# Attention heads projected out in four groups and context keys computed for both batches at once, in a transformer block on one NeuronCore

## The chip, the core and the metric

The kernel runs on one NeuronCore of a Trainium2 chip. The core has four compute engines with queues of their own: TensorE (matrix products, in the profile PE, and PEld for loading its weights), VectorE (DVE), ScalarE (ACT) and GpSimd (POOL). SyncE (SP) only issues DMA transfers. Work is done from an on-chip memory, and matrix products land in eight PSUM banks, which hold 512 float32 numbers in each of 128 partitions. The metric is device time in microseconds; lower is better.

## The reference

A transformer block in float32: layer norm, self-attention, layer norm, attention to a context, layer norm, a gated feed-forward layer, each with its residual.

```python
h = _layernorm(x, ln1_g, ln1_b)
x = _attention(h, h, sa_wq, sa_wk, sa_wv, sa_wo, sa_bo) + x
h = _layernorm(x, ln2_g, ln2_b)
x = _attention(h, cond_emb, ca_wq, ca_wk, ca_wv, ca_wo, ca_bo) + x
h = _layernorm(x, ln3_g, ln3_b)
p = h @ ff_w1 + ff_b1
a, gate = (p[..., :D_FF], p[..., D_FF:])
h = a * jax.nn.gelu(gate, approximate=False) @ ff_w2 + ff_b2
return h + x
```

`x` is 2 x 1024 x 256 and the context 2 x 154 x 192. There are 16 heads of 64 columns, so attention works on 1024 columns between its input projections and the output projection `wo` (1024 x 256). The feed-forward layer is 1024 wide, with a gate of the same width.

## The kernel before

The work is a fixed order of instructions, written out by hand and not reordered by a scheduler. A **unit** is one pair of heads of one batch. There are 16 units, numbered through batch 0 and then batch 1. Token tiles have 128 rows; a batch has eight.

**Self-attention** takes 8 steps a unit, 128 in all. Step `p` does the scores of 128 queries (`scores`, two tiles `s` of two banks each), their maxima on VectorE, the exponents on ScalarE (`exponents`), an exchange of row statistics by four small DMAs (`exchange`), and for earlier steps the scaling on GpSimd, the transposes on VectorE (`turn_groups`) and the sums with the values (`self_values`, tiles `po`). In steps 0, 1, 4 and 5 of a unit `run_work` puts something from a list `work` on TensorE: the projections of the next unit's queries, keys and values (`pq_sa`, `pk_sa`, `pv_sa`), which need two banks each; what is left of the two banks goes to the list `outs`. A third list, `side`, holds small pieces of the next norm, with the tiles of the residual that each needs (`needs`).

**The output projection** adds up heads in PSUM. `out_piece` (L452) takes one half of a batch's heads, four pairs (`HP = NPAIR // 2`), and one token tile: four products into half a bank, then one VectorE addition of 128 x 256 onto the residual. A half can be projected once its four pairs are done, so `self_beside` (L654) hands out pieces from unit 4 on, two tiles a unit; the last half of batch 1 follows in cross-attention, at its step 5. The head outputs of a half lie in a tile `oT`, of which there are two.

**Cross-attention** has three steps a unit, 48 in all (`cross_first`, tiles `sc`). Beside a unit's steps go the queries of a later unit (`cross_queries`), its keys (`cross_keys`, L700: the product of the context of one batch with one pair's weights, two products of 154 columns, then a copy on ScalarE), for every second unit the context values, two output-projection tiles from unit 6 on (`cross_beside`, L858), and the sums (`cross_values`, tiles `poc`) of two units before. Probabilities go through VectorE transposes and then through eight DMAs that regroup them (`cross_regroup`) before the sums can read them. The output projection's weights `wo` have one buffer; those of cross-attention are loaded when self-attention's last piece is done.

**The feed-forward stage** has 64 slots (`gate_slot`, tiles `pa`; `sum_slot`, tiles `pf`). Beside its first slots run what is left of cross-attention's output projection, half of one half and the whole of the next, and the last norm.

PSUM is given out in three pools of two: `ps_s` for scores, `ps_m` (`mm_tile`) and `ps_o` (`sum_tile`). VectorE's additions wait in a list `adds`, ScalarE's and VectorE's copies out of PSUM in a list `stores`; both are emptied at fixed places in each step.

Of the kernel before, what the change touches and what calls it, by code (L numbers as in the profile page):

```python
# [13 lines left out]
P = 128  # L14
# [4 lines left out]
def tile_transformer_block(ctx: ExitStack, tc: tile.TileContext, a: dict, out: bass.AP):  # L19
# [10 lines left out]
    HP = NPAIR // 2  # L30
# [105 lines left out]
    def load_weights(kind, pr, what):  # L136
        if kind == "sa" or what == "q" or what == "k":
            wsl[kind, pr, what] = load_slice(
                f"{kind}_w{what}", pr * P, P, HR if kind == "sa" or what == "q" else CC)
        elif pr % 2 == 0:  # L140
            wsl[kind, pr, what] = load_slice(f"{kind}_w{what}", pr * P, VC, CC)
# [4 lines left out]
    def load_ahead_parts():  # L146
# [10 lines left out]
        def chunk(i):  # L157
            nc.sync.dma_start(out=wo["sa"][:, i, :], in_=w["sa_wo"][i * P:(i + 1) * P, :])

        pieces = ([lambda t=t: tile_of_x(t) for t in tile_order("sa")]  # L160
                  + [lambda i=i: chunk(i) for i in range(NPAIR)])
        slots = [u * 2 * SH + n for u in range(1, HP + 1) for n in (0, 1, 4, 5)]
# [21 lines left out]
    nc.gpsimd.memset(ctxT, 0.0)  # L184

# [131 lines left out]
    def norm_beside(kind, b):  # L317
# [12 lines left out]
        for k in range(NT // n + 3):  # L330
            tiles = tile_order(kind)[k * n:(k + 1) * n]
            needs = [(after, b, half, t) for half in range(2) for t in tiles if after]
# [119 lines left out]
    def out_piece(kind, b, half, t):  # L452

        o = oT[kind, b, half]
        py = spare["out"](f"py_{kind}{b}_{half}_{t}")
        for i in range(HP):
            nc.tensor.matmul(  # L457
                py[:, :D], lhsT=o[:, i, t * P:(t + 1) * P], rhs=wo[kind][:, half * HP + i, :],
                start=(i == 0), stop=(i == HP - 1),
            )  # L460
        xs = xt[b, t // GT][:, t % GT, :]

        def add():
            nc.vector.tensor_tensor(xs, py[:, :D], xs, ALU.add)  # L464
            added.add((kind, b, half, t))

        add.adds = True
        return add

# [184 lines left out]
    def self_beside(ui):  # L654
# [9 lines left out]
        if ui >= HP:  # L664
            ob, oh = divmod((ui - HP) // HP, 2)
            t0 = (ui % HP) * 2
            out_pieces("sa", ob, oh, tile_order("ca")[t0:t0 + 2])
        if ui == 1:
            norm_beside("sa", 1)
        if ui in (HP, HP + 2):  # L670
            add_biases("sa", (ui - HP) // 2)
# [3 lines left out]
    def load_ahead(p):  # L675

        ui, n = divmod(p, 2 * SH)
        for what in "qkv":
            at = {"q": 2, "k": 3, "v": 2 * SH - 1}[what] + 3 * (ui == 0 and what != "v")
            if n != at:  # L680
                continue
# [4 lines left out]
        if p in (SA - 3, SA - 2):  # L686
            load_weights("ca", units[p - SA + 4][1], "kq"[p - SA + 3])
# [6 lines left out]
    def cross_queries(b, pr, m=P, bank=mm_tile):  # L694
        q = qk["ca", b, pr, "q"] = p2.tile([P, S], F32, tag="QT", name=f"q_ca{b}_{pr}")
# [4 lines left out]
    def cross_keys(b, pr, bank=mm_tile):  # L700
        k = qk["ca", b, pr, "k"] = p2.tile([P, S], F32, tag="KT", name=f"k_ca{b}_{pr}")
        pk = bank(f"pk_ca{b}_{pr}")
        for c in range(2):
            nc.tensor.matmul(
                pk[:, :T], lhsT=wsl["ca", pr, "k"][:, c, :],
                rhs=ctxT[:, c, b * TP:b * TP + T], start=(c == 0), stop=(c == 1),
            )
        return lambda: nc.scalar.copy(k[:, :T], pk[:, :T])
# [36 lines left out]
    def cross_pieces(b, pr):  # L745

        return [costing(2, lambda: cross_queries(b, pr, KB)), costing(1, lambda: cross_keys(b, pr)),
                costing(1, lambda: context_values(b, pr))]

    def cross_first(c):  # L750
# [4 lines left out]
        q, k = qk["ca", b, pr, "q"], qk["ca", b, pr, "k"][:, :T]  # L755
# [102 lines left out]
    def cross_beside(ui):  # L858
# [3 lines left out]
        if ui > HP + 1:  # L862
            ob, oh = divmod((ui - HP - 2) // HP, 2)
            t0 = ((ui - HP - 2) % HP) * 2
            out_pieces("ca", ob, oh, (t0, t0 + 1))
        if ui == NU - 4:
# [99 lines left out]
    with tc.manual_schedule():  # L966
# [57 lines left out]
        for p in range(SA):  # L1024
# [10 lines left out]
            flush(adds)  # L1035
            if late:
                late()
            if later and (p < 2 * SH * HP or p % (2 * SH) in (2, 4, 6)):
# [5 lines left out]
            if h == 0 or hg < LAG:  # L1044

                run_work(2 if p < SA - SH else 1, h % 2 or h == 0, sum_tile)
                if p == LAG:
                    load_weights("sa", units[1][1], "v")
            else:
                run(lambda: self_values(h - 1, hg - LAG))  # L1050

        for c in range(CA):
# [5 lines left out]
            if c == SH + 1:  # L1058
                out_pieces("sa", B - 1, 1, tile_order("ca"))
                outs.append(lambda: load_out("ca"))  # L1060
# [12 lines left out]
            elif n == 2:  # L1073
# [116 lines left out]
```

## Time and profile before

| | |
|---|---|
| median of 3 runs | 1136.88 us (1136.82 to 1140.38) |
| profiled execution | 1138.26 us, its span 1136.5 us |
| TensorE busy | 1109.5 us (98%) |
| VectorE busy | 841.2 us (74%) |
| ScalarE busy | 632.0 us (56%) |
| GpSimd busy | 681.2 us (60%) |
| self-attention | 0 to about 717 us |
| cross-attention | about 717 to 936 us |
| feed-forward | about 936 us to the end |

The profile is of one execution. Its span runs from the first to the last instruction; the time of a run has a little more around it. "L457" is line 457 of the kernel. A float32 product is two TensorE instructions, so the four products of an output-projection tile are eight in the profile. A tile is named by its program name without its number (`py_sa` is an output-projection tile of self-attention). [...]

### The profile page before, as it was taken

Reading aid. Unit: us, or ns where it says so; the run is one execution under the profiler, and the core shown is the slowest. Engines: PE = TensorE matmul, PEld = TensorE weight load, DVE = VectorE, ACT = ScalarE, POOL = GpSimd, SP = SyncE. Lnnn points to the kernel's source line nnn. Section 1 sums busy time; section 2 is a strip of 40 time slices with the busy share of each in tenths; the row PEclk is TensorE's granted clock in tenths of the full one; section 3 lists DMA queues with packets and bytes.
Section 4 is the critical chain, followed back from the end, with each engine's and each line's share of the span. In section 5 each row is a group of like instructions: output and inputs, shape, how many; then the busy total and the mean of one; then the engine's idle time right before and its main releaser. Section 6 shows DMA issues by size and latency. Waiting matters only on the chain.

```text
span 1136.5 us, 36749 instructions
## 1 busy us (share of the span) xinstructions
PE 1109.5 (98%) x14372; PEld 689.9 (61%) x14372; DVE 841.2 (74%) x1203; ACT 632.0 (56%) x2046; POOL 681.2 (60%) x1584
## 2 busy tenths in 40 slices
PE   8999999999999999999999999999999999999998
PEld 6444444545545545445455454675777767888887
DVE  4889999898898999899998889767666773222222
ACT  4666666666765666666677666646555552021111
POOL 2777777878777777777777767757554553040000
PEclk9999999999999999999999999999999999999999
DMA  2222122201111111111111010166755542000000
GB/s 83 62 53 49 40 49 50 54 18 40 37 25 41 31 31 45 31 32 40 26 37 40 22 32 12 39 160 167 173 123 123 123 88 57 10 10 10 19 10 19
DMA packets 104911, 59.94 MB, mean 53 GB/s; under 512 B 32090, under 2 KB 95522, under 8 KB 104738
## 3 DMA queue, kind: packets, MB, share of 16 engines
q1 hardware_dynamic: 103506, 56.93, 21.0%
q8 instruction: 114, 1.87, 0.7%
q10 hardware_dynamic: 1232, 0.66, 0.2%
q14 instruction: 59, 0.48, 0.1%
HBM read 27.91 MB, written 2.10 MB: 26 GB/s over the span
## 4 chain that ended last, share of the span: by engine, by line
PE 79%; ACT 6%; DVE 4%; DMA 4%; POOL 3%; SPq 2%; issue 2%; DVEq 0%; POOLq 0%; ACTq 0%
PE po L526 16%; PE s L479 16%; PE pa L921 9%; PE py_sa L457 5%; PE pf L944 5%; PE py_ca L457 5%; ACT p L490 4%; PE pk_sa L353 4%; PE pq_ca L353 4%; PE pv_sa L384 4%; PE poc L839 4%; PE pq_sa L353 3%; PE sc L760 2%; SPq L500 2%; DVE st L641 2%; DMA st<-st 2%
## 5 line engine op out<-in xcount | busy, mean ns | idle before, releaser
L490 ACT ACTIVATE p<-s,st 128x512 f32<-128x512 f32 x512 | 344.8, 686 | 203.2 <-DVE st L641 197.3
L591 POOL TENSOR_SCALAR p<-p,rd,ee 128x512 f32<-128x512 f32 x512 | 385.6, 767 | 45.2 <-DVE rd L587 44.2
L641 DVE TENSOR_REDUCE st<-s 128x2 f32<-128x1024 f32 x256 | 301.2, 1218 | 32.6 <-PE s L479 20.9
L605 DVE STREAM_TRANSPOSE pT<-p 128x1024 f32<-128x1024 f32 x256 | 302.2, 1218 | 0.3 <-POOL p L591 0.3
L479 PE MATMUL s<-k_sa,q_sa 64*32 64x512 f32 x4096 | 252.6, 594 | 13.1 <-ACT p L490 12.5
L526 PE MATMUL po<-pT,v_sa 64*64 64x256 f32 x4096 | 235.8, 379 | 0.4 <-DVE pT L605 0.4
L526 PEld LDWEIGHTS po<-pT,v_sa 64*64 64x64 f32 x4096 | 150.4, 133 | 109.0 <-issue 32.0
L787 POOL TENSOR_SCALAR p<-p,rden 128x154 f32<-128x154 f32 x256 | 96.8, 398 | 89.4 <-DVE rden L784 89.0
L479 PEld LDWEIGHTS s<-k_sa,q_sa 64*32 64x32 f32 x4096 | 66.1, 106 | 135.9 <-issue 62.4
L776 ACT ACTIVATE p<-sc,neg 128x154 f32<-128x154 f32 x256 | 95.9, 401 | 87.3 <-DVE rden L784 82.0
L930 DVE SCALAR_TENSOR_TENSOR u<-pa,cols,gate 128x256 f32<-128x256 f32 x64 | 30.9, 483 | 121.8 <-ACT gate L927 121.8
L921 PE MATMUL pa<-hT_ln,wf 128*128 128x256 f32 x512 | 120.7, 379 | 0.0
L927 ACT ACTIVATE gate<-pa,cols 128x256 f32<-128x256 f32 x64 | 30.3, 474 | 155.3 <-PE pa L921 153.6
L921 PEld LDWEIGHTS pa<-hT_ln,wf 128*128 128x128 f32 x512 | 96.8, 190 | 13.5 <-DVE o_ca L852 0.4
L490 ACT ACTIVATION_READ_ACCUMULATOR p<-s,st 128x1 f32 x512 | 103.9, 203 | 0.0
L384 PEld LDWEIGHTS pv_sa<-sa_wv,hT_ln 64*128 64x128 f32 x1024 | 59.0, 188 | 17.4 <-DMA st<-st 7.5
L514 POOL TENSOR_TENSOR zz<-ee,st 128x8 f32<-128x8 f32 x128 | 25.9, 202 | 66.0 <-ACT ee L512 66.0
L944 PE MATMUL pf<-wf,u 128*128 128x256 f32 x256 | 64.7, 379 | 0.0
L384 PE MATMUL pv_sa<-sa_wv,hT_ln 64*128 64x128 f32 x1024 | 62.8, 276 | 0.6 <-ACT v_sa L393 0.6
L457 PE MATMUL py_ca<-ca_wo,o_ca 128*128 128x256 f32 x256 | 60.9, 387 | 0.9 <-DVE x L464 0.8
L457 PE MATMUL py_sa<-sa_wo,o_sa 128*128 128x256 f32 x256 | 59.5, 385 | 0.0
L765 DVE TENSOR_REDUCE neg<-sc 128x6 f32<-128x924 f32 (+1 forms) x48 | 47.9, 999 | 14.4 <-PE sc L760 14.4
(87 smaller groups left out, 1245.1 us busy)
## 6 DMA issues: line engine op xcount, KB each, us to landing
wf<-pT_ca SPq DMA_DIRECT2D x128, 128.0 KB, 2.4
st<-st SPq DMA_DIRECT2D x512, 1.0 KB, 1.8
v_sa<-v_sa SPq DMA_DIRECT2D x32, 256.0 KB, 3.5
sa_wq<-in_L_xattn_sa_wq_dram SPq DMA_DIRECT2D x32, 128.0 KB, 3.0
sa_wk<-in_L_xattn_sa_wk_dram SPq DMA_DIRECT2D x32, 128.0 KB, 3.0
sa_wv<-in_L_xattn_sa_wv_dram SPq DMA_DIRECT2D x32, 128.0 KB, 3.0
ca_wq<-in_L_xattn_ca_wq_dram SPq DMA_DIRECT2D x32, 128.0 KB, 3.0
wf<-in_L_xattn_ff_w_dram SPq DMA_DIRECT2D x12, 256.0 KB, 3.9
```

Of the source, the lines that this page charges most:

```text
L353: nc.tensor.matmul(pq[r][f:f + m, at:at + n], lhsT=wt[own, c, f:f + m], rhs=h[own, c, t0:t0 + n], start=(c == 0), stop=(c == NH - 1), tile ...
L384: nc.tensor.matmul(pv[r][:, i * P:(i + 1) * P], lhsT=h[own, c, i * P:(i + 1) * P], rhs=wt[own, c, :], start=(c == 0), stop=(c == NH - 1), ...
L457: nc.tensor.matmul(py[:, :D], lhsT=o[:, i, t * P:(t + 1) * P], rhs=wo[kind][:, half * HP + i, :], start=(i == 0), stop=(i == HP - 1),)
L479: nc.tensor.matmul(sc[a4 * KB:(a4 + 1) * KB, j, :], lhsT=q[r, c:c + KB], rhs=k[r, h * HB:(h + 1) * HB], start=True, stop=True, tile_positi ...
L490: nc.scalar.activation(pr[:, j, :], sc[:, j, :], AF.Exp, bias=st[:, 0, 0, i, j:j + 1], accum_out=st[:, 0, 1, i, j:j + 1],)
L526: nc.tensor.matmul(po[a2][j * DH:(j + 1) * DH, :QH // 2], lhsT=v[r, t, e, j * DH:(j + 1) * DH], rhs=pT[r, j * NK + n, :], start=(t == 0 an ...
L591: nc.gpsimd.tensor_scalar(pr[:, j, :], pr[:, j, :], rd[:, c:c + 1], ee[:, 0, c:c + 1], op0=ALU.mult, op1=ALU.mult,)
L605: nc.vector.transpose(halves[h][:, :, c:c + KB], groups.pop(0).rearrange("p j (n k) -> p (j n) k", k=KB))
L641: nc.vector.tensor_reduce(st[:, 0, 0, i, :], sc[i], AX.X, ALU.max, negate=True)
L787: nc.gpsimd.tensor_scalar(pr_[:, j, i, :T], pr_[:, j, i, :T], rden[:, j, i:i + 1], 1.0, op0=ALU.mult, op1=ALU.mult,)
L921: nc.tensor.matmul(pa[:, half, :TF * P], lhsT=w1[:, c, half * DF + f * P:half * DF + (f + 1) * P], rhs=h[:, c, t0 * P:(t0 + TF) * P], star ...
L944: nc.tensor.matmul(sums[blk][i][:, :D], lhsT=sums[blk, "u"][:, f, i * P:(i + 1) * P], rhs=w2[:, f, :], start=(f == 0), stop=(f == NF - 1),)
```

## The change

The heads of a batch are projected out in four groups of two pairs in place of two halves of four. A piece covers two token tiles, each with two products, side by side in one bank, and one VectorE addition of 128 x 512. Pieces begin at unit 2 of self-attention and at unit 4 of cross-attention; of batch 1 one group is left for cross-attention's step 5, and two for the feed-forward slots 0 and 5. In self-attention VectorE does at most one waiting addition a step. The first two weight rows of `wo` are loaded ahead of half of batch 1's token tiles.

The context's keys are computed once a pair for both batches (two products of 320 columns, one ScalarE copy into a tile that stays), in step 5 of self-attention's units 1 to 8; cross-attention no longer computes keys. Their weights are loaded once a pair, in step 6 of a unit (step 4 of unit 0), into a single buffer.

At the end of cross-attention the pieces of its last unit run in the first of its steps. The load of cross-attention's `wo` stands in the last step of unit 2, ahead of that step's regrouping.

```diff
-    HP = NPAIR // 2
+    NQ = 4
+    HP = NPAIR // NQ
...
-        if kind == "sa" or what == "q" or what == "k":
...
+        if (kind, what) == ("ca", "k"):
+            wsl[kind, pr, what] = load_rows(
+                wpool, "ck", f"ca_wk_{pr}", w["ca_wk"][:, pr * P:(pr + 1) * P], CC)
...
-        pieces = ([lambda t=t: tile_of_x(t) for t in tile_order("sa")]
-                  + [lambda i=i: chunk(i) for i in range(NPAIR)])
-        slots = [u * 2 * SH + n for u in range(1, HP + 1) for n in (0, 1, 4, 5)]
+        tiles = [lambda t=t: tile_of_x(t) for t in tile_order("sa")]
+        chunks = [lambda i=i: chunk(i) for i in range(NPAIR)]
+        pieces = tiles[:4] + chunks[:HP] + tiles[4:] + chunks[HP:]
+        slots = [u * 2 * SH + n for u in range(1, 5) for n in (0, 1, 4, 5)]
...
+    kT = const.tile([P, NPAIR, B * TP], F32, tag="kT", name="kT")
...
-    def out_piece(kind, b, half, t):
+    def out_piece(kind, b, g, t):
 
-        o = oT[kind, b, half]
-        py = spare["out"](f"py_{kind}{b}_{half}_{t}")
-        for i in range(HP):
-            nc.tensor.matmul(
-                py[:, :D], lhsT=o[:, i, t * P:(t + 1) * P], rhs=wo[kind][:, half * HP + i, :],
-                start=(i == 0), stop=(i == HP - 1),
-            )
-        xs = xt[b, t // GT][:, t % GT, :]
+        o = oT[kind, b, g]
+        py = spare["out"](f"py_{kind}{b}_{g}_{t}")
+        for e in range(2):
+            for i in range(HP):
+                nc.tensor.matmul(
+                    py[:, e * D:(e + 1) * D], lhsT=o[:, i, (t + e) * P:(t + e + 1) * P],
+                    rhs=wo[kind][:, g * HP + i, :], start=(i == 0), stop=(i == HP - 1),
+                )
+        xs = xt[b, t // GT][:, t % GT:t % GT + 2, :].rearrange("p t d -> p (t d)")
 
         def add():
-            nc.vector.tensor_tensor(xs, py[:, :D], xs, ALU.add)
+            nc.vector.tensor_tensor(xs, py, xs, ALU.add)
...
+    def out_order(kind):
+
+        return [t for t in tile_order("ff" if kind == "ca" else "ca") if t % 2 == 0]
...
         if ui >= HP:
-            ob, oh = divmod((ui - HP) // HP, 2)
+            ob, og = divmod((ui - HP) // HP, NQ)
             t0 = (ui % HP) * 2
-            out_pieces("sa", ob, oh, tile_order("ca")[t0:t0 + 2])
+            out_pieces("sa", ob, og, out_order("sa")[t0:t0 + 2])
...
+        if n == (4 if ui == 0 else 6) and ui < NPAIR:
+            load_weights("ca", ui, "k")
...
-    def cross_keys(b, pr, bank=mm_tile):
-        k = qk["ca", b, pr, "k"] = p2.tile([P, S], F32, tag="KT", name=f"k_ca{b}_{pr}")
-        pk = bank(f"pk_ca{b}_{pr}")
+    def context_keys(pr):
+
+        pk = sum_tile(f"pk_{pr}")
         for c in range(2):
             nc.tensor.matmul(
-                pk[:, :T], lhsT=wsl["ca", pr, "k"][:, c, :],
-                rhs=ctxT[:, c, b * TP:b * TP + T], start=(c == 0), stop=(c == 1),
+                pk[:, :B * TP], lhsT=wsl["ca", pr, "k"][:, c, :], rhs=ctxT[:, c, :],
+                start=(c == 0), stop=(c == 1),
             )
-        return lambda: nc.scalar.copy(k[:, :T], pk[:, :T])
+        return lambda: nc.scalar.copy(kT[:, pr, :], pk[:, :B * TP])
...
         if ui > HP + 1:
-            ob, oh = divmod((ui - HP - 2) // HP, 2)
+            ob, og = divmod((ui - HP - 2) // HP, NQ)
             t0 = ((ui - HP - 2) % HP) * 2
-            out_pieces("ca", ob, oh, (t0, t0 + 1))
-        if ui == NU - 4:
+            out_pieces("ca", ob, og, out_order("ca")[t0:t0 + 2])
+        if ui == NU - 5:
             norm_beside("ff", 0)
...
-            flush(adds)
+            if adds:
+                adds.pop(0)()
...
+                ui, n = divmod(p, 2 * SH)
+                if n == SH + 1 and 0 < ui <= NPAIR:
+                    run(lambda: context_keys(ui - 1))
...
             if c == SH + 1:
-                out_pieces("sa", B - 1, 1, tile_order("ca"))
-                outs.append(lambda: load_out("ca"))
+                out_pieces("sa", B - 1, NQ - 1, out_order("sa"))
...
-            elif n == 2:
-                for i, what in ((2, "k"), (1, "v")):
-                    if 1 < ui + i < NU:
-                        load_weights("ca", units[ui + i][1], what)
-            if c == 0:
-                run(lambda: cross_keys(*nxt))
+            elif n == 2 and nxt and ui:
+                load_weights("ca", nxt[1], "v")
             flush(adds)
             then = cross_first(c)
-            if n == 1 and ui > 1 and nxt:
-                run(lambda: cross_keys(*nxt, sum_tile))
-                stores.insert(0, stores.pop())
...
                 run(lambda: self_values(2 * NU - 1, 1))
-                run(lambda: cross_keys(*nxt, sum_tile))
             elif n == 0 and ui:
                 if nxt:
                     run(lambda: cross_queries(*nxt))
+                else:
+                    run_work(2, 0)
                 run_work(0, 1)
...
-                run_work(0, 1, sum_tile if ui == HP - 1 else None)
-                if len(outs) > 2:
+                run_work(0, 1, sum_tile if ui == HP + 1 else None)
+                if c == SH + 1:
                     run_work(2, 0)
+                elif ui == HP:
+                    load_out("ca")
...
             if k == 0:
-                out_pieces("ca", B - 1, 0, range(NT - 2 * TF, NT))
-            if k == 1:
-                run_work(2, 0)
-                flush(adds)
+                out_pieces("ca", B - 1, NQ - 2, out_order("ca"))
...
             if k == len(CG) + 2:
-                out_pieces("ca", B - 1, 1, range(NT))
+                out_pieces("ca", B - 1, NQ - 1, out_order("ca"))
...
-            run_work(2, 1)
+
+            run_work(0 if k == 1 else 2, 1)
```

## The prediction

> **What bounds the kernel now.** I read the page first, then TensorE per unit, then its matmuls in order of time. The page (busy time; then tenths in 40 slices):
>
> ```profile
> PE 1109.5 (98%) x14372; PEld 689.9 (61%) x14372; DVE 841.2 (74%) x1203; ACT 632.0 (56%) x2046; POOL 681.2 (60%) x1584
> ...
> PE   8999999999999999999999999999999999999998
> ...
> DVE  4889999898898999899998889767666773222222
> ```
>
> TensorE (PE) is busy everywhere and VectorE (DVE) nearly so for the first 60%; averages don't say which one sets the pace. So the windows of single self-attention units, cut at their first score matmul: units 1, 2, 3, then 10 and 13 (window, PE, PEld, DVE, ACT, POOL busy, clock, DMA):
>
> ```profile
> 60.87:103.91 43.04, 40.92 (x708) 20.19 (x704) 38.96 (x45) 27.24 (x83) 32.01 (x72) 1.00 0.21 52
> 103.91:148.57 44.66, 41.37 (x709) 20.17 (x705) 39.75 (x46) 28.56 (x87) 33.42 (x77) 1.00 0.19 44
> 148.57:192.19 43.62, 41.27 (x713) 19.84 (x709) 39.75 (x46) 29.96 (x91) 32.31 (x71) 1.00 0.19 46
> ...
> 455.07:498.51 43.44, 43.44 (x724) 22.69 (x720) 39.67 (x48) 28.29 (x82) 32.68 (x73) 1.00 0.15 34
> 586.58:630.61 44.03, 44.03 (x729) 23.14 (x725) 39.07 (x44) 30.20 (x88) 32.85 (x75) 1.00 0.15 33
> ```
>
> Units 1 to 3 leave PE idle; from unit 4 on it never stops. The chain of waits through unit 10 (start, us, what):
>
> ```profile
> 455.14 1.88 PE s L479 x32
> 457.02 3.43 PE pq_sa L353 x64
> ...
> 467.32 3.61 PE po L526 x64
> ...
> 478.30 3.77 PE pv_sa L384 x64
> ...
> 483.95 3.65 PE py_sa L457 x16
> ```
>
> A unit is eight score sets (8 x 1.88), four po pieces (4 x 3.61), pq and pk (3.43 each), pv (3.77) and two out-projection tiles (3.65): 43.8, against 43.44 measured. So here every microsecond of matmul counts. Units with a norm's transposes take 0.58 more (44.03).
>
> [...] The row that decides is the sum of pieces that equals the period, with no gap: in this order of work PE is full. [...]
>
> Cross-attention and the start of the feed-forward stage, PE in order of time (start, us, matmul, idle before it and who ended it):
>
> ```profile
> 794.93 0.86 PE L839 MATMUL poc<-wf,v_ca 64*64 64x256 f32 x10 [1.73 <-DVE hT_ln L282]
> ...
> 846.17 0.79 PE L704 MATMUL pk_ca<-ctxT,ca_wk 96*128 96x154 f32 x4
> 846.80 3.62 PE L457 MATMUL py_ca<-ca_wo,o_ca 128*128 128x256 f32 x16
> ...
> 925.92 1.06 PE L760 MATMUL sc<-k_ca,q_ca 64*128 64x154 f32 x12 [1.80 <-ACT p L776]
> ...
> 927.67 5.02 PE L457 MATMUL py_ca<-ca_wo,o_ca 128*128 128x256 f32 x16
> ...
> 942.80 3.72 PE L457 MATMUL py_ca<-ca_wo,o_ca 128*128 128x256 f32 x16 [0.81 <-DVE x L464]
> ```
>
> PE runs without gaps from unit 6 to unit 14 (27.0 us for two units), has gaps around units 4 and 5 and between 924 and 950, and is full again (170.00 of 170.00 us) from 963 to 1133.
>
> **The change, part by part.** A py matmul costs 0.216 (3.45 for x16), a pk_ca set of four 0.63 (846.17 to 846.80).
>
> *Self-attention, out-projection from unit 2.* Units 2 and 3 now get two pieces of two tiles, 16 instructions, 3.65 us each, and one value projection in place of two halves. They then hold what unit 13 holds. With the keys (below) each is 44.03 + 1.08 = 45.1, against 44.66 and 43.62: **+1.9**. Their weight rows are brought forward in SP's queue by half a unit and batch 1's later tiles back by as much; each is still at least half a unit ahead of its reader.
>
> *Context keys.* Four instructions with N=320 in place of 154. At 256 columns one takes 0.216, so 0.27 here: 1.08 a unit, in units 1 to 8 at step 5. Unit 1 has idle PE (2.1 us, at just these steps): 0. Units 4 to 8: **+5.4**. ScalarE's copy (294 ns at 154, 372 at 256, so some 430) goes ahead of the next step's exponents; po, queued behind it for the bank, starts only after 1.9 us of scores. One 96 KB load of SP a unit, at a step that had none, falls between two exchanges; the wait on its single buffer ends a step earlier.
>
> *Adds twice as wide.* 64 as before. DVE issues two of 256 in 0.72 and a 1024-wide reduce in 1.18, so 512 takes about 0.63: two take 1.26, not 0.72, one in each of steps 6 and 7 rather than both in 6. DVE waits 0.38 and 0.54 for the denominators in those steps, which covers them; the next q projection, queued behind the bank of the second add, starts 0.3 after its end. I take **+0.2**, ends 0 and 7 (0.5 in each of 14 units if that cover is missing).
>
> *Cross-attention, units 0 and 1.* Of the two key sets, the one at 717 lies ahead of a po at 728.16 that waits 0.41 for DVE's transposes: 0. The one at 736: **-0.7**.
>
> *Units 2 to 5.* Out go four key sets (-2.5) and four single sa tiles of the old last half (-7.2: x16 in unit 2's third step, x16 in unit 3). In come two ca groups' tiles in units 4 and 5 (+6.9), which fill the waits there (783 and 795: split poc runs of 3.6 and 5.1 us instead of 2.75: -3.75). New in unit 3: the 1 MB ca_wo load now stands just ahead of the eight regrouping DMAs that poc waits for. SP needs 5.3 to 6.3 us to issue those eight; the packets show ca_wo filling the DMA engines for 4.5 us. Unit 3 has only 5.9 us of PE work between two poc runs (sc 0.7, sc 0.9, pq 3.4, sc 0.9), so poc waits: between 0 and 4.5, I take +2.3. Sum **-4.3**.
>
> *Units 6 to 14.* Nine key sets: **-5.7**. SP loses 0.5 a unit of issue. Two odd units with a transpose find the first, wider add late for poc's bank: **+0.8** (0 to 2).
>
> *Unit 15 and the start of the feed-forward.* Unit 15's two pieces now run in its first step, into the 1.80 gap. Gone too should be the 0.81 and 0.61 (949.88) behind the crowd of single tiles at its second slot. And the clock: the 16 py instructions at 927.67 took 5.02 instead of 3.45. The granted clock in stretches of 3.4 us:
>
> ```profile
> 923.20:926.60 3.40, 1.60 (x25) 1.37 (x24) 3.40 (x8) 1.70 (x9) 2.22 (x7) 1.00 0.94 200
> 926.60:930.00 3.40, 3.40 (x16) 2.79 (x15) 3.15 (x8) 3.40 (x19) 2.53 (x10) 0.57 0.49 104
> ```
>
> A stretch with PE at 1.60 of 3.40 and then half a clock. [...] The row shows the fall right after a half-idle stretch, so I count the 1.57 too. Together 4.8, less 0.6 for new waits (the exponents of the last steps, the regrouping, 7.6 us from release to landing, now with 6.4 us of work ahead of unit 14's poc): **-4.2**.
>
> *Feed-forward.* Out-projection instructions fall from 96 to 64; PE is full: 32 x 0.216 = **-6.9**. These 32 are the ones that units 2 and 3 took in, passed on by way of cross-attention.
>
> Sum: 1.9 + 5.4 + 0.2 - 0.7 - 4.3 - 5.7 + 0.8 - 4.2 - 6.9 = **-13.5**. Made the other way: matmul work on the path is nearly unchanged (14 key sets out, 9.0; eight in, 8.6; out-projection equal), so almost all is idle PE filled: 9 in units 1 to 3, the rest around cross-attention's ends. The profiled execution took 1138.26 with a span of 1136.5; the median of the runs is 1136.88, and I take the difference from that: **1123.4 us**.
>
> **Rivals.**
> - *Cross-attention has a floor below PE*: without the keys, the exponent chain, the regrouping or SP sets the pace. For it: SP is issuing nearly all the time from 783 to 800. Against: DVE is at 17.6 of 27.1 and ACT at 15.9 in the steady pairs. Two thirds of nine key sets lost, and a fall of the clock in unit 3's new wait: +7, 1130.5.
> - *The additions to self-attention hide*[...]: 7.5 less, 1116. Against: the sum of pieces.
> - *Work is only moved, no idle time is filled*: the new places wait as the old did, and 9.0 - 8.6 remain: 1136.5.
> - *Slower: VectorE becomes the pace of self-attention.* Units 1 to 3 took 43.0 to 44.7 with PE idle, bound by the loop score, maximum, exponent. If the wider add, in front of the next maximum, stretches that loop, PE waits in all 14 units with out-projection. At 0.96 us a unit the gain is gone; at 1.26, 1141. Against: in unit 12 (with a norm) the exponents end 0.8 to 2.4 us before the scores that need their bank; only at step 0 of unit 8 have I seen 0.24.
>
> **How the numbers follow.** Likeliest 0.58 (own range 1119 to 1128, from the ends of the waits above); floor 0.16; hidden 0.10; only moved 0.08; slower 0.08. A change under 0.3% (3.4 us) can't be told from none. Faster 0.84, same 0.08, slower 0.08. The range, 1115 to 1131, holds the first three but for their edges and leaves out the last two.
>
> **What would show it.** Units 2 and 3 at 45.1, 4 to 8 at 44.5 to 45.3, 9 to 15 unchanged; cross-attention pairs at 25.8, not 27.0; a gap on poc near 760 with ca_wo ahead of it; no half clock near 927; py out of the feed-forward after two slots instead of four. Wrong if units 9 to 15 grow (the adds), if pairs stay at 27, or if the end of cross-attention keeps its gaps.

## The result, and the profile after

| | before | after |
|---|---|---|
| median, us | 1137.90 (1136.82 to 1140.38) | 1130.72 (1130.03 to 1131.45) |
| ratio, with 95% interval | 1 | 0.9934 (0.9914 to 0.9954) |
| profiled execution: time, span | 1138.26, 1136.5 | 1130.48, 1128.7 |

The changed kernel is 7.2 us faster (0.66%, 0.5 to 0.9% by the interval). When it was run again on another chip, beside the kernel before, it took 1130.86 us and the ratio was 0.9923 (0.9907 to 0.9940). The kernel before took 1136.88 us in the runs that the prediction started from, and its median was 1137.9 to 1139.9 in the later comparisons; so ratios are compared below where kernels were run on different chips. The predicted 1123.4 us was too low. The measured 1130.7 lies inside the range of 1115 to 1131, by 0.3 us, and outside the 1119 to 1128 that the likeliest reading allowed itself.

The page of the changed kernel: busy times, then TensorE's and VectorE's tenths of 40 slices.

```profile
PE 1110.2 (98%) x14340; PEld 690.0 (61%) x14340; DVE 856.5 (76%) x1205; ACT 631.2 (56%) x2032; POOL 681.0 (60%) x1584
...
PE   8999999999999999999999999899999999999998
...
DVE  4889889898888988999989989977767875312222
```

TensorE is as busy as before (1110.2 us, it was 1109.5) in a span 7.8 us shorter: the gain is idle time, as the prediction said. One slice in the middle, the 26th (705 to 734 us), now shows 8. That is where something went wrong.

The windows of self-attention units 1, 2, 3, 6, 7, 10 and 13 (window, its length, busy time of PE, PEld, DVE, ACT, POOL, the granted clock, DMA share and rate):

```profile
62.39:105.16 42.77, 41.92 (x712) 20.16 (x708) 38.96 (x45) 27.59 (x84) 31.66 (x70) 1.00 0.20 50
105.16:151.20 46.04, 45.60 (x728) 24.45 (x724) 40.74 (x47) 29.22 (x88) 33.42 (x78) 1.00 0.20 48
151.20:196.36 45.16, 45.16 (x732) 24.63 (x728) 40.80 (x48) 30.42 (x89) 32.87 (x75) 1.00 0.19 46
...
287.59:332.70 45.11, 45.11 (x732) 23.90 (x729) 39.45 (x43) 29.26 (x87) 33.94 (x75) 1.00 0.15 35
332.70:377.22 44.52, 44.52 (x728) 23.48 (x724) 39.44 (x43) 28.25 (x83) 33.92 (x76) 1.00 0.15 35
466.07:509.64 43.57, 43.57 (x724) 23.62 (x721) 40.46 (x48) 28.38 (x83) 33.35 (x77) 1.00 0.14 33
597.91:641.94 44.03, 44.03 (x729) 23.15 (x725) 39.44 (x44) 30.33 (x89) 32.87 (x74) 1.00 0.15 33
```

Units 2 and 3 had TensorE idle for 3.3 and 2.4 us and are full now but for 0.44 us in unit 2, yet they are longer (44.66 and 43.62 before). Units 6 and 7 carry one key set each (two products, four instructions) and are 1.08 and 1.0 us longer (44.03 and 43.51 before). Unit 13 is what it was.

TensorE in order of time through cross-attention and the first feed-forward slots (start, us, line, matmul, shapes, count; in brackets the idle time before it and who ended it):

```profile
773.10 0.65 PE L851 MATMUL poc<-wf,v_ca 64*64 64x256 f32 x4 [1.56 <-DMA wf<-pT_ca]
774.22 0.86 PE L851 MATMUL poc<-wf,v_ca 64*64 64x256 f32 x10 [0.47 <-DMA wf<-pT_ca]
...
776.63 0.87 PE L851 MATMUL poc<-wf,v_ca 64*64 64x256 f32 x10 [0.65 <-ACT p L788]
...
927.43 3.72 PE L463 MATMUL py_ca<-ca_wo,o_ca 128*128 128x256 f32 x16
...
935.81 1.99 PE L933 MATMUL pa<-hT_ln,wf 128*128 128x256 f32 x8 [0.20 <-ACT p L788]
...
961.54 3.62 PE L463 MATMUL py_ca<-ca_wo,o_ca 128*128 128x256 f32 x16
...
968.45 3.62 PE L463 MATMUL py_ca<-ca_wo,o_ca 128*128 128x256 f32 x16
```

The first three lines are unit 3's wait for the regrouped probabilities. The other lines are the end of cross-attention: the out-projection at 927 takes 3.72 us where it took 5.02, the gap of 1.80 us ahead of it is gone, and the last four pieces, two to a run of 16 instructions, stand in feed-forward slots 5 and 6. The granted clock over that end, and over 3.4 us near 717:

```profile
924.00:927.40 3.40, 3.40 (x60) 2.44 (x52) 2.13 (x5) 0.00 (x0) 0.00 (x0) 1.00 0.42 92
927.40:930.80 3.40, 3.40 (x18) 2.96 (x16) 3.40 (x8) 2.52 (x13) 3.04 (x9) 1.00 0.80 174
717.00:720.40 3.40, 3.40 (x36) 0.58 (x40) 3.15 (x5) 1.35 (x5) 2.17 (x7) 0.60 0.01 1
```

The clock stays at 1.00 at the end of cross-attention. It falls near 717 instead, in the last unit of self-attention, which nothing in the prediction touched: 0.60 is the mean of this window, and the trace has the clock at 0.50 from 717.68 to 721.09. Below, such a stretch is called a half clock.

The whole difference of the two profiled spans, cut at the same instructions:

| stage | before, us | after, us | difference | predicted |
|---|---|---|---|---|
| start, to the first scores | 17.67 | 17.96 | +0.29 | 0 |
| self-attention, units 0, 1 | 86.24 | 87.20 | +0.96 | 0 |
| units 2, 3 | 88.27 | 91.20 | +2.93 | +1.9 |
| units 4 to 8 | 219.44 | 225.37 | +5.93 | +5.4 |
| units 9 to 14 | 263.20 | 264.22 | +1.02 | +0.2 |
| unit 15 | 42.90 | 43.74 | +0.84 | 0 |
| cross-attention, units 0, 1 | 23.73 | 22.63 | -1.10 | -0.7 |
| units 2 to 5 | 56.83 | 54.00 | -2.83 | -4.3 |
| units 6 to 14 | 124.87 | 120.21 | -4.66 | -4.9 |
| unit 15, and slots 0 to 4 | 36.93 | 31.44 | -5.49 | -4.2 |
| slots 5 to 62 | 168.63 | 161.72 | -6.91 | -6.9 |
| slot 63 to the end | 7.75 | 8.99 | +1.24 | 0 |
| sum | 1136.5 | 1128.7 | -7.8 | -13.5 |

Not every row here is the change, and rows move between executions. When the changed kernel was profiled again, the last stretch took 7.76 us, unit 0 took 43.54 (in the profile above it has a half clock near 35 us) and unit 9 took 43.48. But units 10 and 11 were longer there, units 2 to 8 took 1.5 us more, and the span was 1128.9 us all the same. So a row of less than about 1 us can't be booked to a cause from one profile, while some 5.7 us are missing in both. The experiments went after the parts that have places and names.

### The profile page after: what moved, and what is told of

Its sections match the earlier page's. It is cut to its first block, busy times and chain, and to the rows that moved or that the text cites. A ratio compares the mean times of both kernels' runs of the same rounds, so it can differ in the third digit from the quotient of the medians.

```text
span 1128.7 us, 36667 instructions
## 1 busy us (share of the span) xinstructions
PE 1110.2 (98%) x14340; PEld 690.0 (61%) x14340; DVE 856.5 (76%) x1205; ACT 631.2 (56%) x2032; POOL 681.0 (60%) x1584
## 4 chain that ended last, share of the span: by engine, by line
PE 86%; ACT 4%; DVE 3%; DMA 3%; POOL 2%; SPq 1%; issue 1%; DVEq 0%; POOLq 0%; ACTq 0%
PE po L536 18%; PE s L489 18%; PE pa L933 10%; PE py_ca L463 5%; PE pf L956 5%; PE py_sa L463 5%; PE pk_sa L358 4%; PE pq_ca L358 4%; PE pq_sa L358 4%; PE pv_sa L389 4%; PE poc L851 4%; PE sc L772 3%; ACT p L500 3%; DMA st<-st 2%; DVE st L651 1%; SPq L510 1%
## 5 line engine op out<-in xcount | busy, mean ns | idle before, releaser
L463 PEld LDWEIGHTS py_sa<-sa_wo,o_sa 128*128 128x128 f32 x256 | 47.3, 190 | 17.8 <-issue 7.0
```

The source lines that it names most:

```text
L463: nc.tensor.matmul(py[:, e * D:(e + 1) * D], lhsT=o[:, i, (t + e) * P:(t + e + 1) * P], rhs=wo[kind][:, g * HP + i, :], start=(i == 0), st ...
```

## Experiments

My theory after reading the two traces: the groups do what they should, and the keys don't pay. In self-attention they cost their full matmul time and a wait on top, and by leaving the last unit they opened a gap there that halves the clock. Rivals: the groups themselves fell short; the loss is the load of cross-attention's output weights in unit 3; the keys hide and the loss is elsewhere.

### The groups alone

The context keys go back to where they were, one batch at a time: two sets in self-attention's last unit, fourteen beside cross-attention.

```diff
...
-                ui, n = divmod(p, 2 * SH)
-                if n == SH + 1 and 0 < ui <= NPAIR:
-                    run(lambda: context_keys(ui - 1))
...
+            if n == 1 and ui > 1 and nxt:
+                run(lambda: cross_keys(*nxt, sum_tile))
+                stores.insert(0, stores.pop())
...
+                run(lambda: cross_keys(*nxt, sum_tile))
```

> Output projection in four groups, keys computed in cross-attention as before. If the gain is idle TensorE time filled by out-projection (units 2 and 3, the ends of cross-attention) and the keys are a trade of 9 us against 9 us, this kernel is as fast as the changed one or faster: units 4 to 8 back at 43.5 to 44.0 us, a pair of cross-attention units back at 27.0, the key matmuls at the end of self-attention back; sum about 1128 to 1132. If the keys are what brings the gain, it loses most of it: 1135 or more.

Measured: 1131.24 us (1127.35 to 1132.52), ratio 0.9922 (0.9895 to 0.9948): what the whole change gives, within intervals of half a per cent. The profiled execution, at 1127.35 us, was the fastest of its four. The windows of self-attention units 2, 3, 6 and 7 of this kernel:

```profile
103.58:147.54 43.96, 43.96 (x724) 23.40 (x720) 39.85 (x46) 28.26 (x85) 33.18 (x76) 1.00 0.19 45
147.54:192.09 44.55, 44.55 (x728) 24.27 (x724) 41.51 (x49) 30.79 (x92) 33.18 (x77) 1.00 0.18 45
...
280.34:324.37 44.03, 44.03 (x728) 23.14 (x724) 39.45 (x43) 29.15 (x86) 33.95 (x76) 1.00 0.14 33
324.37:367.82 43.45, 43.45 (x725) 22.73 (x721) 39.45 (x43) 27.58 (x82) 33.99 (x76) 1.00 0.15 34
```

Out-projection in units 2 and 3, two pieces each, costs -0.7 and +0.9 us: it lies in what was idle. Units 6 and 7 are back at the length before. Against this kernel the keys of both batches cost 11.9 us in self-attention (711.75 from the first scores to cross-attention's first, 699.84 here) and save 10.2 in cross-attention (22.63 + 54.00 + 120.21, against 23.78 + 57.21 + 126.04). Of the 11.9 us, 1.6 are in unit 0, which holds no keys and had the half clock near 35 us (the mean clock from 34 to 40 us was 0.72, and 1.00 with the groups alone); without it the cost is 10.3. So the keys bring nothing that can be seen, and the gain is that of the rest: the groups, with the changes at the end of cross-attention and in the loads, which no run takes apart.

### The keys twice

Each set of key products is done twice. The second pass starts the sum anew, since its first product has `start` set, so the keys are the same and only work is added.

```diff
-        for c in range(2):
+        for c in (0, 1, 0, 1):
```

> The changed kernel with every key product of self-attention issued twice (8 instructions in place of 4; the result is the same). If TensorE is full in these units, units 2 to 8 grow by 1.08 us each and unit 1 by less: 7 to 8.6 us more in all. If the additions hide[...], the time doesn't change.

Measured: 1135.46 us, ratio 0.9969 (0.9959 to 0.9979), 4 to 5 us above the changed kernel and less than the 7 to 8.6 expected. Its units 6 and 7:

```profile
288.64:335.24 46.60, 46.60 (x736) 24.61 (x732) 39.45 (x43) 29.40 (x87) 34.09 (x76) 1.00 0.15 33
335.24:380.84 45.60, 45.60 (x732) 24.24 (x728) 39.45 (x43) 28.07 (x83) 34.16 (x76) 1.00 0.15 34
```

Four more instructions lengthen unit 7 by 1.08 us (44.52 to 45.60) and unit 8 by the same; unit 6 by 1.5. PEld is at 24.24 of 45.60 us in unit 7, just over half: weight loading was idle for the other half, and the added products cost their full length all the same. This refutes the prediction's rival that the additions hide. Over units 1 to 8 the doubling costs 6.5 us (359.4 to 365.9) and not 8.6: in units 2 to 5 it covers a wait, the next point, and unit 1 had idle time.

### The keys one step earlier

With the groups alone, steps 5 and 6 of units 2 to 8 take 5.53 and 5.49 us. In the changed kernel step 5 takes 6.61, the 1.08 of the four instructions more. But in units 2, 4 and 5 step 6 grew too, to 6.53, 6.25 and 5.75. TensorE at these steps of unit 2, and ScalarE in unit 4:

```profile
138.01 1.24 PE L717 MATMUL pk<-ctxT,ca_wk 96*128 96x320 f32 x4
139.18 1.95 PE L489 MATMUL s<-k_sa,q_sa 64*32 64x512 f32 x32
141.06 0.65 PE L536 MATMUL po<-pT,v_sa 64*64 64x256 f32 x4
142.11 3.67 PE L536 MATMUL po<-pT,v_sa 64*64 64x256 f32 x60 [0.40 <-ACT kT L721]
```

```profile
231.68 1.09 ACT L266 ACTIVATE xn_ln<-x,off_ln,rstd_ln 128x256 f32<-128x256 f32 x2 [1.69 <-DVE off_ln L252]
232.68 0.40 ACT L721 COPY kT<-pk 128x320 f32<-128x320 f32 x1
```

po needs the bank that pk holds, and the copy that frees it is done late: in ScalarE's queue it stands behind the norm's scaled rows, which wait 1.69 us for VectorE's offsets. The units bear this out. From the start of the key products to that of the copy it takes 3.64, 2.65, 3.36 and 2.86 us in units 2 to 5, and step 6 is longer by 1.04, 0.05, 0.76 and 0.26: each time by what goes beyond 2.6 us. In units 6 and 7, with no such rows ahead of the copy, it takes 1.3 us and step 6 stays at 5.49. The experiment puts the keys at step 4, where no rows of a norm follow.

```diff
-                if n == SH + 1 and 0 < ui <= NPAIR:
+                if n == SH and 0 < ui <= NPAIR:
```

> The changed kernel with the context keys one step earlier, in step 4 of units 1 to 8, so that their copy on ScalarE is not queued behind the norm's scaled rows. If that queue makes po wait in step 6 (0.40, 0.76 and 0.26 us in units 2, 4 and 5), those waits vanish and 1.5 us are gained in units 2 to 5. If the bank is late for another reason, they stay or move to step 5.

Measured: 1128.29 us, ratio 0.9903 (0.9883 to 0.9923). The same po in this kernel:

```profile
138.31 1.95 PE L489 MATMUL s<-k_sa,q_sa 64*32 64x512 f32 x32
140.19 3.68 PE L536 MATMUL po<-pT,v_sa 64*64 64x256 f32 x64
```

It runs as one piece, and step 6 is 5.49 us in units 2 to 8. Units 2 to 5 fall from 182.4 to 180.7 us in all; in units 7 and 8, where no wait was, nothing is gained (44.72 us each, 44.52 before). The time fell by some 2.5 us, with intervals that overlap; the steps carry the verdict.

### The output weights after the regrouping

In unit 3 of cross-attention the 1 MB load of `ca_wo` stands in SP's queue ahead of the eight transfers that regroup the probabilities (start, us, line, transfer; of the changed kernel):

```profile
764.95 0.54 SPq L121 DMA_DIRECT2D ca_wo<-in_L_xattn_ca_wo_dram  x1
765.58 6.94 SPq L832 DMA_DIRECT2D wf<-pT_ca  x8
```

Here it is issued behind them:

```diff
-                elif ui == HP:
-                    load_out("ca")
             cross_regroup(c)
+            if c == len(CG) * HP + 2:
+                load_out("ca")
```

> The changed kernel with the 1 MB load of cross-attention's output weights issued just behind the regrouping transfers of that step, not ahead of them. If that load holds up the regrouping, the wait of poc in unit 3 (about 3.8 us in all near 771 to 778) falls to under 1 and the kernel gains 2.5 to 3.5 us. If the wait is a floor of SP's issue or of the chain of exponents, unit 3 stays at 13.0 us and the time doesn't change.

Measured: 1130.53 us, ratio 0.9923 (0.9904 to 0.9943): no gain. Unit 3 falls from 13.01 to 10.74 us, and unit 4 grows from 14.36 to 16.48, for what now stands behind the load is late:

```profile
780.33 3.91 PE L358 MATMUL pq_ca<-hT_ln,ca_wq 64*128 64x512 f32 x15 [1.22 <-DMA ca_wq<-in_L_xattn_ca_wq_dram]
```

The load costs some 2 us whichever transfer stands behind it. It has to be cut up or be early.

### The output weights in eight rows

Both stages' weights use one tile. A row of 128 KB is loaded as soon as self-attention has read its row for the last time: six beside its last units, two behind the regrouping in cross-attention.

```diff
-        wo["sa"] = const.tile([P, NPAIR, D], F32, tag="wo", name="sa_wo")
+        wo["sa"] = wo["ca"] = const.tile([P, NPAIR, D], F32, tag="wo", name="sa_wo")
...
+        rows_at = [12 * 2 * SH, 12 * 2 * SH + 1, 14 * 2 * SH, 14 * 2 * SH + 1, SA - 4, SA - 3]
...
-                elif ui == HP:
-                    load_out("ca")
             cross_regroup(c)
+            if c in (len(CG) * HP + 2, len(CG) * HP + 4):
+                load_row(NPAIR - 2 + (c - len(CG) * HP) // 4)
```

> The changed kernel with cross-attention's output weights loaded in eight rows of 128 KB as self-attention's last groups free them, six of them before cross-attention, into the same tile. If the 1 MB of data is what holds up the regrouping and then the query weights, poc no longer waits near 771 and no later wait takes its place: units 3 and 4 take 24.5 to 25.5 us together in place of 27.4, 2 to 3 us gained. If the issuing queue or the exponents set that stretch, it stays at 27.

Measured: 1129.15 us, ratio 0.9905 (0.9890 to 0.9920). SP issues the same eight transfers in 5.28 us, not 6.94, and what is left of the wait in unit 3 is another's:

```profile
765.89 5.28 SPq L832 DMA_DIRECT2D wf<-pT_ca  x8
```

```profile
774.83 1.35 PE L851 MATMUL poc<-wf,v_ca 64*64 64x256 f32 x14 [0.88 <-ACT q_ca L373]
```

Units 3 and 4 together take 25.40 us, against 27.37 in the changed kernel's first profile and 26.99 when it was run again: the load's price in the changed kernel is 1.6 to 2.0 us. Behind it a wait of 0.88 us on ScalarE's copy of the queries comes to light, where 0.65 on ScalarE's exponents stood before; the expectation had no later wait.

### The changed kernel again, and the context values one step later

The last unit of self-attention, in the changed kernel, against the kernel before (one fence each):

```profile
709.51 1.99 PE L733 MATMUL pv_ca<-ca_wv,ctxT 96*128 96x256 f32 x8
...
716.96 3.30 PE L489 MATMUL s<-k_sa,q_sa 64*32 64x512 f32 x32 [2.88 <-ACT p L500]
720.19 4.10 PE L536 MATMUL po<-pT,v_sa 64*64 64x256 f32 x64
```

```profile
700.51 1.09 PE L479 MATMUL s<-k_sa,q_sa 64*32 64x512 f32 x16 [1.34 <-ACT p L490]
...
705.54 1.09 PE L479 MATMUL s<-k_sa,q_sa 64*32 64x512 f32 x16 [0.68 <-ACT p L490]
```

The list of pieces that beside this unit's steps go to TensorE had a key set in it before (at 698). Without it the context values come up one step earlier, and step 5 has nothing between two sets of scores: one gap of 2.88 us in place of 1.34 and 0.68. After it 32 score instructions take 3.30 us and not 1.95: that is the half clock at 717. This experiment puts a piece that does nothing where the keys were, so that the values return to step 5; beside it the changed kernel ran once more.

```diff
-        return [costing(2, lambda: cross_queries(b, pr, KB)), costing(1, lambda: context_values(b, pr))]
+        return [costing(2, lambda: cross_queries(b, pr, KB)), costing(1, lambda: None),
+                costing(1, lambda: context_values(b, pr))]
```

> The changed kernel with the context values put back to step 5 of unit 15, where they stood before the keys that were ahead of them were taken away (an empty piece takes their place). If the single TensorE gap of 2.88 us in that unit, which the advance of the values made out of smaller gaps, is what halves the clock near 717, then the gap splits into pieces of about 2 us and less, the half clock there is gone, unit 15 takes 42.9 us or less in place of 43.7 and the time falls by 0.8 to 1.8. If the half clock has another cause it stays.

> The changed kernel itself, beside the next three on one chip, as their base: 1130 to 1131 us.

Measured: 1130.72 us, ratio 0.9917 (0.9902 to 0.9932), against 1130.86 and 0.9923 (0.9907 to 0.9940) of the changed kernel again: the same. The edit missed what it was for. The gap is shorter, but not split as it was before, and the half clock is still there:

```profile
712.07 3.49 PE L489 MATMUL s<-k_sa,q_sa 64*32 64x512 f32 x32 [2.06 <-ACT p L500]
```

Unit 15 falls from 43.65 to 42.47 us, and cross-attention's unit 1 takes 0.8 of that back (13.57 to 14.34). The mean clock over this execution is 0.997. The changed kernel's second profile shows the gap of 2.88 us again, and a mean clock of 0.58 in the 3.40 us behind it.

### Work in the gap

The changed kernel, with six more key products of 320 columns in step 5 of the last unit. They go into a bank that nothing reads, so they add work and change no output.

```diff
+                if p == SA - SH + 1:
+                    fill = sum_tile("fill")
+                    for c in (0, 1, 0, 1, 0, 1):
+                        nc.tensor.matmul(
+                            fill[:, :B * TP], lhsT=wsl["ca", NPAIR - 1, "k"][:, c, :],
+                            rhs=ctxT[:, c, :], start=(c == 0), stop=(c == 1))
```

> The changed kernel with six more key products (320 columns, of the last pair's weights, into a bank that nothing reads: added work, the outputs unchanged) in step 5 of unit 15, where TensorE stood idle for 2.88 us before the scores. It isolates the idle gap from everything else that the 1122.5 us version had. Theory, the gap of 2.9 us brings the half clock at 717: six products of 0.27 us a pass fill 1.6 to 3.2 us of the gap, no half clock is seen between 710 and 725 us, unit 15 falls from 43.7 to 42.0 to 42.9, and the time by about 1 us, to 1129.5 to 1130. Rival, the half clock comes from something else at this place: it is seen within 5 us of the scores of this step all the same, and unit 15 is 43.7 or longer.

Measured: 1129.06 us (1127.86 to 1130.49), ratio 0.9913 (0.9895 to 0.9930). TensorE there, and at the next wait:

```profile
713.87 3.50 PE L1068 MATMUL fill<-ctxT,ca_wk 96*128 96x320 f32 x12
717.30 1.95 PE L489 MATMUL s<-k_sa,q_sa 64*32 64x512 f32 x32
719.18 3.68 PE L536 MATMUL po<-pT,v_sa 64*64 64x256 f32 x64
...
740.06 3.68 PE L536 MATMUL po<-pT,v_sa 64*64 64x256 f32 x64 [1.41 <-DVE pT L615]
```

With 3.4 us of products in the gap the scores take 1.95 us again, and the clock is 1.00 in every window from 690 to 755 us. So the idle gap is the cause of the half clock here: nothing else was changed. Work that is added makes unit 15 1.3 us shorter (43.74 to 42.45). But in this profile the gain doesn't reach the end: TensorE is ahead of VectorE's transposes then and waits 1.41 us for them at 740, cross-attention's unit 1 grows from 13.56 to 15.06, and the mean clock over the execution is 0.998, so the clock fell at some other place. By the medians the kernel is 1.7 us faster than the changed one; the intervals of the ratios overlap.

### All three repairs, and the groups with the rows

The keys of the first five pairs at step 4; those of the last three in step 5 of unit 15, where they fill the gap (their weights in three buffers in place of one); the output weights in rows, as above.

```diff
-                wpool, "ck", f"ca_wk_{pr}", w["ca_wk"][:, pr * P:(pr + 1) * P], CC)
+                wpool, f"ck{pr % 3}", f"ca_wk_{pr}", w["ca_wk"][:, pr * P:(pr + 1) * P], CC)
...
-                if n == SH + 1 and 0 < ui <= NPAIR:
+                if n == SH and 0 < ui <= NPAIR - 3:
                     run(lambda: context_keys(ui - 1))
+                if p == SA - SH + 1:
+                    run(lambda: context_keys(NPAIR - 3, mm_tile))
+                    run(lambda: context_keys(NPAIR - 2, mm_tile))
+                    run(lambda: context_keys(NPAIR - 1))
...
```

> The changed kernel with the three remedies together: output weights in rows, keys in step 4 of units 1 to 5, the keys of the last three pairs in step 5 of unit 15, in its TensorE gap. If TensorE is full in units 6 to 8 and idle in unit 15, units 6 to 8 return to 43.5 to 44.0 (3.2 us), units 2 to 5 lose their waits (1.5), units 3 and 4 of cross-attention gain 2 to 3, and the half clock near 717 goes: 1121 to 1124. If the exponents of unit 15 are delayed by three more copies on ScalarE, unit 15 grows instead by up to 2.

Measured: 1122.51 us (1121.63 to 1123.35), ratio 0.9846 (0.9831 to 0.9861), faster than both kernels: 17 us below the kernel before, about twice what the change itself gave (9 us on the same chip). Its last unit of self-attention:

```profile
709.10 3.50 PE L717 MATMUL pk<-ctxT,ca_wk 96*128 96x320 f32 x12
712.53 1.95 PE L489 MATMUL s<-k_sa,q_sa 64*32 64x512 f32 x32
```

Three key sets, 3.24 us of work, lie in the gap, and unit 15 takes 42.49 us. Units 6 to 8 are back at 44.03, 43.69 and 43.58.

Are the keys worth anything in this version? The next kernel is that of the groups alone, with the keys one batch at a time as in the kernel before, and the edit of the rows on top (the part of the rows):

```diff
-        wo["sa"] = const.tile([P, NPAIR, D], F32, tag="wo", name="sa_wo")
+        wo["sa"] = wo["ca"] = const.tile([P, NPAIR, D], F32, tag="wo", name="sa_wo")
...
+            if p in rows_at:
+                load_row(rows_at.index(p))
...
```

> Four groups and the output weights of cross-attention in eight rows, with the context keys left where they were in the kernel before (half of each pair in units 1 to 7 of self-attention, half in cross-attention). It asks whether the keys of both batches at once are worth anything in the version that took 1122.5 us. Theory, keys are worth their filling of unit 15 alone: the groups alone ran in 1131.2, and the rows took 1.6 to 2.0 us off units 3 and 4 in the changed kernel, so about 1129 to 1130 here, with pairs of cross-attention at 27.0 us, units 6 to 8 of self-attention at 43.5 to 44.0 and unit 15 at 42.9, and the 1122.5 us version stays 6 to 8 us ahead, of which its pairs of cross-attention should hold about 6 (units 6 to 14). Rival, the keys are worth nothing at all and the 1122.5 us came from groups and rows: about 1123 to 1124 here.

(The expectation names a wrong place for the keys of the kernel before: they lie in self-attention's last unit, two sets, and in cross-attention, fourteen.) Measured: 1127.79 us (1126.61 to 1129.97), ratio 0.9905 (0.9889 to 0.9921). So the keys of both batches, well placed, are worth 5 to 7 us (5.3 by the medians, 6.7 by the ratios, 0.9846 against 0.9905, with intervals apart). By the profiles they save 9.0 us in cross-attention (195.15 against 204.11, over its units 0 to 14) and cost 3.0 in self-attention (705.67 against 702.67), or 4.5 if unit 0 is left out, which has the same instructions in both and took 44.38 us in the second, with a mean clock of 0.998 over that execution, and 42.91 in the first, with 1.00. In the change as it was made they cost 11.9, or 10.3 without unit 0. The rows are worth 2.9 us in units 2 to 5 here (57.21 to 54.34).

## Why the prediction was right, and its size too large

The direction and its mechanism held: idle TensorE time in units 2 and 3, around cross-attention's ends and in the crowd of single tiles was filled. The size was -13.5 for a measured -7.2 (-9.0 when both kernels were run again). That the time still fell inside the range is in part luck: it is 0.3 us from the range's edge, and errors of both signs went into it. Point by point:

- **Out-projection from unit 2: right.** Predicted +1.9 with the keys. Without the keys it is +0.2 (88.51 against 88.27), and the keys' 2 x 1.08 would make it +2.4; the half microsecond is a longer step 2 of unit 3 (5.95 us, 5.47 before).
- **The keys' matmul time: right to the hundredth.** 1.08 a unit, in units 2 to 8. The rival that would have made it nothing is refuted for these units by doubling the products: 1.08 us more in unit 7, with PEld at 24.24 of 45.60.
- **The step that failed: "po, queued behind it for the bank, starts only after 1.9 us of scores."** The cover is there, but I had counted only the copy's own length against it, not what stands ahead of the copy in ScalarE's queue. The norm's rows, waiting for VectorE, took up the cover and more: 2.1 us in steps 6 of units 2, 4 and 5. Moving the keys by one step took it away.
- **Missing from the sum: what leaves a list moves what stands behind it.** I took the keys out of cross-attention's side, at -0.63 a set, and left unit 15 of self-attention "unchanged"; the set at 698 stands nowhere in the sum. There the context values moved up by a step and left a gap of 2.88 us; that this gap brought the half clock is shown by filling it (a clock of 0.50 with the gap, 1.00 with the filler). Unit 15 cost +0.84. The filled unit is 1.3 us shorter, and in that profile a wait for VectorE in the next stage took 1.5 back.
- **Wider adds: right, near enough.** Steps 6 and 7 of units 6 to 8 took 5.49 us before and after, and unit 13 44.03. The groups alone, with the same wider additions, took 263.5 us in units 9 to 14, against 263.2 before: that is the +0.2. The changed kernel took 264.2 and, again, 264.5; what the rest is stays open.
- **Keys out of cross-attention: a little less than said.** A pair of units fell from 27.04 to 25.99, 0.52 a unit and not 0.63. That fits four instructions at 0.13, which is 154 columns at the rate of the 320-column ones (0.27); the 0.63 read off two starts was 0.1 too much.
- **Units 2 to 5: -2.8 for -4.3.** The new wait behind the 1 MB load was sized well (2.3; the rows showed 1.6 to 2.0 in the changed kernel and 2.9 without the keys). What was overrated is the filling. The -3.75 for the split poc runs doesn't come out of its own figures, which give 0.85 + 2.35 = 3.2; behind the wait for the load another of 0.65 to 0.9 us on ScalarE appeared, and four key sets gave 0.4 us less.
- **The end of cross-attention: better, -5.5 for -4.2.** The half clock near 927, which I had put down to a half-idle stretch, is gone with that stretch (the clock is 1.00 in both windows from 924.00 to 930.80), and so are all but 0.2 us of the waits that I had allowed for.
- **Feed-forward: -6.91 for -6.9.** TensorE is full there (busy for all 183.89 us from 935.81 to 1119.70), and 32 instructions at 0.216 are what it lost.
- **The second way of the sum: also off.** "9 in units 1 to 3" is 7.8 by the windows shown (2.1 + 3.3 + 2.4), and only units 2 and 3 received output projections.

Of the rivals, "the additions hide" is refuted by the doubled keys. "Cross-attention has a floor" gave nearly the measured time, 1130.5, but by luck: its pairs did fall by 1.05 us, where 1.26 was the most they could by my figure, and its +7 is more than its own parts, two thirds of nine key sets (3.8) and one half clock (1.6). "VectorE becomes the pace" is refuted by units 12 to 14 at 44.03. "Only moved" holds for one part of the change, the keys: work of equal cost in another place.

## What to carry to other kernels

Where TensorE is the bound, work that is moved pays only if it lands in a gap that is there in the trace; the same key products were worth nothing at a full step and 5 to 7 us when some of them lay in an idle one. When a piece leaves a list of work, follow every list that it was in: what stood behind it moves up, and a hole can appear somewhere else. And a cover is to be counted from the queue's point of view: not "the copy takes 0.4 us", but when the copy comes up in its engine's queue, behind what, and whom that waits for.

## What the runs showed of the hardware

The half clock was the surprise: in these traces the length of a gap doesn't tell where it comes. In the changed kernel a gap of 1.59 us ahead of the scores at 34.61 was followed by a clock of 0.50 from 35.00 to 38.42 us, and the gap of 2.88 by one from 717.68 to 721.09; the gap of 1.56 at 773.10 was not (1.00 from 773.06 to 776.46). In the kernel before, two gaps of nearly one length ended differently. These are the 3.40 us behind the gap of 1.73 us and behind that of 1.80 (window, its length, busy time of PE, PEld, DVE, ACT, POOL, the granted clock, DMA):

```profile
794.93:798.33 3.40, 3.40 (x54) 2.37 (x56) 1.59 (x4) 0.78 (x5) 1.29 (x4) 1.00 0.81 228
925.90:929.30 3.40, 3.38 (x20) 2.95 (x21) 3.15 (x7) 2.81 (x15) 2.53 (x9) 0.68 0.69 145
```

A longer gap with no half clock behind it, in unit 3 of cross-attention with the groups alone:

```profile
764.05 0.65 PE L846 MATMUL poc<-wf,v_ca 64*64 64x256 f32 x4 [2.20 <-DMA wf<-pT_ca]
```

```profile
764.10:767.50 3.40, 2.89 (x32) 1.51 (x36) 1.19 (x3) 2.21 (x12) 3.40 (x9) 1.00 1.03 259
```

And behind the gap of 2.06 us with the context values one step later:

```profile
712.06:715.46 3.40, 3.39 (x32) 0.60 (x32) 3.17 (x4) 1.40 (x5) 2.26 (x8) 0.54 0.04 5
```

So 1.59, 1.80 and 2.06 us were followed by a half clock, 1.56, 1.73 and 2.20 were not. The length alone doesn't sort these six, and what else does is left open here. What was shown is that the half clock at 717 came with its gap and went when the gap was filled.

The price was 1.57 us at 927 in the kernel before (5.02 for 3.45) and 1.8 us at 717 in the changed one (3.30 and 4.10 for 1.95 and 3.68), on top of the gap. In the version with all repairs, and with the filler in the gap, no gap in the second half of self-attention's last unit exceeds 0.25 us, and the clock there stayed at 1.00. With all repairs the mean clock over the profiled execution is 1.00.
